# Gathers with a bound: leaving out the rows of dropped choices in a two-layer convolution kernel

## The chip, the core and the metric

The kernel runs on one core of a Trainium2 chip. The metric is the device time of one execution in microseconds (us). Before the change it is 5500.93 us, the median of three runs (5497.88 to 5509.63). The profiled execution took 5513.8 us. In the profile PE is TensorE's matrix products and PEld its weight loads, DVE is VectorE, ACT is ScalarE, POOL is GpSimd and SP is SyncE; L853 is line 853 of the kernel.

## What is computed

The input x has 32 images of 128 channels and 56 x 56 pixels, all in float32. Layer 0 is a depthwise 7 x 7 convolution, a normalisation over the channels, and a mixture of experts over all 32 x 3136 = 100,352 pixels ("tokens"). Layer 1 is a dilated 3 x 3 convolution followed by two-dimensional Fourier transforms, an attention over channels and a gate. What matters here is how layer 0 drops work and how its result comes back (the reference, cut):

```python
logits = xf @ Wg + bg
topv, topi = jax.lax.top_k(logits, 2)            # two experts of eight for each token
wts = jax.nn.softmax(topv, axis=-1)
order = jnp.argsort(-wts[:, 0])                  # the surest tokens come first
cap = int(1.25 * T / 8)                          # 15,680 rows for each expert
...
keep = pos < cap                                 # pos: place of the choice in its expert's queue
slot = jnp.where(keep, tiF * cap + pos, E * cap) # a dropped choice points past the end
...
yf = jnp.concatenate([y.reshape(E * cap, C), jnp.zeros((1, C), y.dtype)], axis=0)
contrib = yf[slot] * gate[:, None]               # there stands a row of zeros
...
return input + x_skip + moe_out                  # layer 1 starts from this sum
```

There are 200,704 choices and at most 8 x 15,680 = 125,440 are kept, so at least 37.5% of the choices are dropped and add nothing.

## The kernel before, in words

The work goes in three stretches.

In the first one (about 0 to 965 us) TensorE computes the depthwise convolution, VectorE and ScalarE normalise, and the router's logits and choices are made. The normalised tokens go to a table xf in HBM, in row blocks: a row block is eight image rows of two images, seven columns of 128 tokens, and there are 112 of them.

In the second one (about 965 to 3250 us) the experts run one after the other. For each expert VectorE makes the list of its tokens, GpSimd gathers their rows from xf (L674, tile xg, 128 rows each and 64 in the last gather of an expert, since 15,680 = 122 x 128 + 64), TensorE and ScalarE compute the two dense layers, and SyncE stores the gated rows in a table yf in HBM. Beside that VectorE adds up, for every token, where its two rows stand in yf: slot1 and slot2. They begin at NSLOT = 125,440, and a choice that is dropped keeps that value. yf has NSLOT + 1 rows, and the last one is zero (zrow, L389 to L391).

In the third one (from about 3250 us) layer 1 runs over 16 pairs of images. For each pair `front` builds the input of layer 1 and its convolution, and `back` does the transforms, the attention and the gate of the pair before. TensorE alternates between them: after each piece of `back` the driver draws pieces of `front` in proportion to the work done, beginning after the first sixth of `back` (LEAD, L1139). A pair has NB = 7 row blocks, and a row block goes through three small functions:

- `gather(r)` loads the 896 x 128 values of xf (tile xs, one plain load on SyncE's queue), and gathers the rows of yf that slot1 and slot2 name, into two tiles y of 128 x 7 x 128. A gather takes one column of 128 indices and fetches 128 rows of 512 bytes, so a row block has 14 of them, and the whole stretch has 112 x 14 = 1568 (L853). They are all issued by GpSimd, one after the other.
- `total(r)` adds both y tiles to xs on VectorE (L867).
- `place(r)` turns xs to channel-first on TensorE (L875) and adds it to the padded input image xp on VectorE (L880).

`feed(rb)` calls place for its own block, total for the next one and gather for the block three ahead. The tiles y come from a pool of four buffers, so two row blocks are in flight, and the gathers of block r + 2 must wait until `total(r)` has read its y tiles. A program that lays out the instructions on each engine keeps every engine's instructions in one fixed order, and each engine waits in that order. So an instruction that waits holds up all that stand behind it on its engine. ScalarE's instructions in this stretch are the Gelu of the convolution (feat, L906), the evacuations of transform results from PSUM (T at L945, Q at L1020), squares, roots and absolute values (sr, si, oa, ob), and one small root for the attention (nrm, L989).

Of the kernel before, what the change touches and what calls it, by code (L numbers as in the profile page):

```python
# [29 lines left out]
F32 = mybir.dt.float32  # L30
# [7 lines left out]
C = 128  # L38
# [12 lines left out]
NB = H // P8  # L51
# [20 lines left out]
def conv_seq_kernel(ctx: ExitStack, tc: tile.TileContext, t: dict, out: bass.AP, dbg: dict):  # L72
    nc = tc.nc
# [4 lines left out]
    NSLOT = E * cap  # L78
# [5 lines left out]
    dram = ctx.enter_context(tc.tile_pool(name="dram", bufs=1, space=DRAM))  # L84
# [15 lines left out]
    nc.vector.memset(eps6, 1.0e-6)  # L100

    xf = dram.tile([J * 128, PITCH], F32, name="xf")
    yf = dram.tile([NSLOT + 1, C], F32, name="yf")
    xfv = xf.rearrange("(j p) c -> p j c", p=128)


# [7 lines left out]
    with tc.tile_pool(name="a1", bufs=1) as a1, tc.tile_pool(name="a2", bufs=2) as a2, tc.tile_pool(  # L114
        name="a3", bufs=3
# [214 lines left out]
        for g in range(HI // 2):  # L330
            y = a2.tile([128, TG, C], F32, name="y")
# [31 lines left out]
    with tc.tile_pool(name="b1", bufs=1) as b1, tc.tile_pool(name="b2", bufs=2) as b2, tc.tile_pool(  # L363
        name="c1", bufs=1
# [21 lines left out]
            )  # L386
            nc.vector.tensor_tensor(out=b2v[:, e], in0=b2v[:, e], in1=lsB, op=ALU.mult)

        zrow = c1.tile([1, C], F32, name="zrow")  # L389
        nc.vector.memset(zrow, 0.0)  # L390
        nc.sync.dma_start(out=yf[NSLOT : NSLOT + 1, :], in_=zrow)  # L391

        blocks = b1.tile([128, U, NC], F32, name="blocks")
        for u in range(U):
            nc.vector.tensor_scalar(
                out=blocks[:, u, :], in0=iota[:, :NC], scalar1=float(-u), scalar2=None, op0=ALU.add
# [4 lines left out]
            out=token, in0=iota, scalar1=-128.0, scalar2=128.0, op0=ALU.add, op1=ALU.mult  # L401
# [440 lines left out]
    rows = {}  # L842

    def gather(r):
        if r >= NRB:
            return
        xs = d3.tile([128, NB, C], F32, name="xs")
        nc.sync.dma_start(out=xs, in_=xfv[:, r * NB : (r + 1) * NB, :C])
        ys = []
        for s in (slot1, slot2):  # L850
            y = d4.tile([128, NB, C], F32, name="y")
            for m in range(NB):
                nc.gpsimd.indirect_dma_start(  # L853
                    out=y[:, m, :],
                    out_offset=None,
                    in_=yf,
                    in_offset=bass.IndirectOffsetOnAxis(ap=s[:, r * NB + m : r * NB + m + 1], axis=0),
                )
            ys.append(y)
        rows[r] = xs, ys  # L860

    def total(r):
        if r >= NRB:
            return
        xs, ys = rows[r]
        for y in ys:
            nc.vector.tensor_tensor(out=xs, in0=xs, in1=y, op=ALU.add)  # L867

    def place(r, xps):
        xs, rb = rows.pop(r)[0], r % NB  # L870
        for m0 in range(0, NB, 4):
            nm = min(4, NB - m0)
            pt = bank("pxs")
            for m in range(nm):
                nc.tensor.transpose(pt[:, m * 128 : (m + 1) * 128], xs[:, m0 + m, :], ident)  # L875
            pv = pt[:, : nm * 128].rearrange("p (m i r s) -> p i r m s", m=nm, i=2, r=P8)
            for i in range(2):
                px = interior(xps[i], rb * P8, P8)[:, :, m0 * P8 : (m0 + nm) * P8]
                px = px.rearrange("p r (m s) -> p r m s", m=nm)
                nc.vector.tensor_tensor(out=px, in0=px, in1=pv[:, i], op=ALU.add)  # L880

    def front(pr, xps, feat):


        for i in range(2):
            nc.sync.dma_start(out=xps[i], in_=t["xp"][pr + i * HI])

        def feed(rb):
            r = pr * NB + rb
            place(r, xps)  # L890
            total(r + 1)
            gather(r + 3)

        def taps(pf, g, k0):
            for k in range(k0, k0 + 3):
                o = ((k // 3) * 3 + 8 * g) * RP + (k % 3) * 3
                for i in range(2):
                    nc.tensor.matmul(  # L898
                        pf[i * DD : (i + 1) * DD, : 8 * W],
                        lhsT=cw[:, k, :],  # L900
                        rhs=xps[i][:, o : o + 8 * RP].rearrange("p (h w) -> p h w", w=RP)[:, :, :W],
                        start=(k == 0),
                        stop=(k == 8),
                    )
            if k0 == 6:
                nc.scalar.activation(  # L906
                    feat[:, 8 * g * W : 8 * (g + 1) * W], pf[:, : 8 * W], AF.Gelu, scale=bsc, bias=bsh
                )

        feed(0)  # L910
        yield NB * 64
        for g in range(NB):
            if g + 1 < NB:
                feed(g + 1)
                yield NB * 64
            pf = psumf.tile([128, 512], F32, name="pf")
            for k0 in (0, 3, 6):
                taps(pf, g, k0)
                yield 3 * 8 * W


# [219 lines left out]
    for r in range(3):  # L1141
        gather(r)
# [9 lines left out]
    for w in front(0, *this):  # L1152
        pass
    for pr in range(NI // 2):
        then, steps = None, iter(())
        if pr + 1 < NI // 2:
            then = pair()
            steps = front(pr + 1, *then)
        made = fed = 0
        for w in back(pr, *this):  # L1160
            made += max(w, 0)
            goal = max(0, made - LEAD) * FRONT // (MAIN - LEAD)
            if w < 0:
                goal = max(goal, fed - w * 3 * 8 * W)
            while fed < goal:
                f = next(steps, None)
                if f is None:
                    break
                fed += f
        for w in steps:  # L1170
            pass
        this = then
# [137 lines left out]
```

## Time and profile before

| stretch, us | what runs | PE busy | ACT busy | POOL busy |
|---|---|---|---|---|
| 0 to 965 | depthwise convolution, routing | 664.17 | 467.99 | 11.44 |
| 965 to 3250 | experts | 2012.97 | 683.39 | 963.78 |
| 5367 to 5513.8 | end of the last pair | 123.31 | 78.14 | 0.20 |

The stretches between, 3250 to 5367 us, hold layer 1 with its gathers. They are shown word for word in the prediction. Busy time is the time in which an engine works on an instruction; the page's groups give for each kind of instruction its line, engine, operation, tile and number, then busy time and the mean duration of one in ns, and after the second bar the idle time of the engine just before these instructions with what ended it. "Issue" there means that the engine waited for nothing that the profile shows.

The software queue that carries the gathers is shown among the DMA queues as q0, with 81,664 packets and 175.18 MB in the whole execution: 103 MB of y rows and 72 MB of xg rows. Over the whole span TensorE is busy for 84%, VectorE for 56%, GpSimd for 47% and ScalarE for 38%.

### The profile page before, as it was taken

Reading aid. Unit: us, or ns where it says so; the run is one execution under the profiler, and the core shown is the slowest. Engines: PE = TensorE matmul, PEld = TensorE weight load, DVE = VectorE, ACT = ScalarE, POOL = GpSimd, SP = SyncE. Lnnn points to the kernel's source line nnn. Section 1 sums busy time; section 2 is a strip of 40 time slices with the busy share of each in tenths; the row PEclk is TensorE's granted clock in tenths of the full one; section 3 lists DMA queues with packets and bytes.
Section 4 is the critical chain, followed back from the end, with each engine's and each line's share of the span. In section 5 each row is a group of like instructions: output and inputs, shape, how many; then the busy total and the mean of one; then the engine's idle time right before and its main releaser. Section 6 shows DMA issues by size and latency. Waiting matters only on the chain.

```text
span 5513.8 us, 85629 instructions
## 1 busy us (share of the span) xinstructions
PE 4653.0 (84%) x32850; PEld 3226.8 (59%) x32850; DVE 3073.9 (56%) x6927; ACT 2097.5 (38%) x3595; POOL 2613.8 (47%) x2564
## 2 busy tenths in 40 slices
PE   6777675189988989899999965899999999899898
PEld 6666554166666667667776743555555555555556
DVE  4767776746565656454453322555555555555556
ACT  2544556023322323233333310444444444444445
POOL 0000000053535343445454447777777777777770
PEclk9888887589999999999999987999999999999999
DMA  9999995222222222222222243444444444444441
GB/s 258 247 242 244 241 233 132 50 66 60 69 54 66 57 62 61 63 66 71 69 70 73 73 120 74 118 126 127 123 123 124 125 123 123 125 128 125 123 121 42
DMA packets 616217, 634.09 MB, mean 115 GB/s; under 512 B 166145, under 2 KB 540546, under 8 KB 611714
## 3 DMA queue, kind: packets, MB, share of 16 engines
q1 hardware_dynamic: 332418, 395.64, 25.6%
q0 software_dynamic: 81664, 175.18, 14.8%
q10 hardware_dynamic: 201728, 57.81, 5.4%
q8 instruction: 260, 4.26, 0.3%
q14 instruction: 147, 1.20, 0.1%
HBM read 454.98 MB, written 173.41 MB: 114 GB/s over the span
## 4 chain that ended last, share of the span: by engine, by line
POOL 28%; PE 25%; issue 19%; DVE 7%; DMA 6%; ACT 2%; ACTq 0%; POOLq 0%; DVEq 0%; SPq 0%
POOL y L853 17%; POOL xg L674 10%; PE py L718 6%; PE ph L708 5%; PE pf L898 4%; PE pm L942 4%; DMA xg<-xf,ids 3%; DMA y<-yf,slot 2%; PE pt L934 2%; PE pg L966 1%; ACT y L181 1%; PE psa L136 1%; PE pxt L680 1%; DVE junk L419 1%; DVE y L187 1%
## 5 line engine op out<-in xcount | busy, mean ns | idle before, releaser
L853 POOL DMA_INDIRECT y<-yf,slot x1568 | 1638.6, 1045 | 527.7 <-issue 501.0
L674 POOL DMA_INDIRECT xg<-xf,ids x984 | 963.8, 979 | 1338.4 <-PE pxt L680 490.0
L711 ACT ACTIVATE hT<-ph,b1t 128x512 f32<-128x512 f32 (+1 forms) x992 | 676.1, 682 | 1428.8 <-PE ph L708 1402.6
L718 PEld LDWEIGHTS py<-W,hT 128*128 128x128 f32 x7872 | 950.8, 195 | 224.7 <-issue 155.1
L718 PE MATMUL py<-W,hT 128*128 128x128 f32 x7872 | 998.2, 281 | 75.4 <-DVE yo L731 69.8
L708 PE MATMUL ph<-xT,W 128*128 128x512 f32 (+1 forms) x1984 | 903.9, 595 | 0.2 <-DVE xT L694 0.2
L898 PE MATMUL pf<-xp,cw 128*64 128x448 f32 x4032 | 885.9, 566 | 0.9 <-DVE xp L880 0.8
L867 DVE TENSOR_TENSOR xs<-xs,y 128x896 f32<-128x896 f32 x224 | 244.4, 1091 | 644.7 <-DMA y<-yf,slot 591.9
L898 PEld LDWEIGHTS pf<-xp,cw 128*64 128x64 f32 x4032 | 289.0, 141 | 465.9 <-issue 439.7
L708 PEld LDWEIGHTS ph<-xT,W 128*128 128x128 f32 x1984 | 359.9, 193 | 336.4 <-issue 329.7
L136 PE MATMUL psa<-xt,wt 112*64 112x98 f32 x8192 | 413.1, 262 | 83.2 <-DMA wt<-in_wt_dram 74.9
L685 DVE SCALAR_TENSOR_TENSOR gat<-xg 128x4 f32<-128x4 f32 (+2 forms) x256 | 42.1, 164 | 785.0 <-DMA xg<-xf,ids 782.4
L136 PEld LDWEIGHTS psa<-xt,wt 112*64 112x64 f32 x8192 | 389.4, 146 | 121.4 <-issue 67.0
L936 DVE COPY mid<-pt 112x512 f32<-112x512 f32 (+3 forms) x480 | 305.3, 660 | 229.7 <-PE pt L934 229.0
L290 POOL MEMSET meta<- 128x1568 f32 x8 | 11.2, 1404 | 887.1 <-DMA xf<-meta 451.5
L181 ACT ACTIVATE y<-y,nb,sd 128x128 f32<-128x128 f32 x784 | 307.9, 482 | 119.1 <-issue 70.2
L945 ACT COPY T<-pm 128x464 f32<-128x464 f32 (+2 forms) x240 | 124.7, 520 | 404.7 <-PE pm L942 404.7
L144 DVE TENSOR_TENSOR y<-psa,dwbB 128x392 f32<-128x392 f32 x256 | 142.7, 563 | 232.8 <-PE psa L136 232.7
L731 DVE TENSOR_TENSOR yo<-py,b2t 128x512 f32<-128x512 f32 (+2 forms) x256 | 169.8, 666 | 112.1 <-PE py L718 111.3
L198 PE MATMUL pyt<-ident,y 128*128 128x128 f32 x784 | 137.8, 347 | 92.0 <-DVE nb L174 57.9
L680 PE MATMUL pxt<-ident,xg 128*128 128x128 f32 (+1 forms) x984 | 195.2, 280 | 11.0 <-DMA xg<-xf,ids 10.8
L1033 PE MATMUL pim<-feat,meanw 128*128 128x448 f32 x224 | 126.4, 651 | 92.2 <-ACT gt L1088 92.2
(376 smaller groups left out, 6185.1 us busy)
## 6 DMA issues: line engine op xcount, KB each, us to landing
xt<-in_x_dram SPq DMA_DIRECT2D x128, 784.0 KB
yf<-yo SPq DMA_DIRECT2D x240, 256.0 KB
xp<-in_xp_dram SPq DMA_DIRECT2D x32, 1832.0 KB
wt<-in_wt_dram SPq DMA_DIRECT2D x128, 448.0 KB
xs<-xf SPq DMA_DIRECT2D x112, 448.0 KB
xf<-y ACTq DMA_DIRECT2D x48, 1024.0 KB
y<-yf,slot POOLq DMA_INDIRECT x1568
out_dram<-oa SPq DMA_DIRECT2D x224, 112.0 KB
```

The lines of the kernel that those rows point to most:

```text
L136: nc.tensor.matmul(ps[h * 64 : (h + 1) * 64, c * TG : (c + 1) * TG], lhsT=wt[:, c4 + c, b, :], rhs=xv[:, c4 + c, h, :, b * NB : b * NB + N ...
L181: nc.scalar.activation(yi, yi, AF.Identity, scale=sd[:, i : i + 1], bias=nb[:, i : i + 1])
L674: nc.gpsimd.indirect_dma_start(out=xg[:n, q, :], out_offset=None, in_=xf, in_offset=bass.IndirectOffsetOnAxis(ap=ids[:n, c0 + q : c0 + q + ...
L680: nc.tensor.transpose(pt[:, q * 128 : q * 128 + n], xg[:n, q, :C], ident[:n, :n])
L708: nc.tensor.matmul(ph[:, :ns], lhsT=W1[:, e, f * C : (f + 1) * C], rhs=xT[:, :ns], start=True, stop=True)
L711: nc.scalar.activation(hT[:, f, :ns], ph[:, :ns], AF.Gelu, bias=b1t[:, e, f : f + 1])
L718: nc.tensor.matmul(py[:n, q * C : (q + 1) * C], lhsT=hT[:, f, q * 128 : q * 128 + n], rhs=W2[:, e, f, :], start=(f == 0), stop=(f == FF // ...
L853: nc.gpsimd.indirect_dma_start(out=y[:, m, :], out_offset=None, in_=yf, in_offset=bass.IndirectOffsetOnAxis(ap=s[:, r * NB + m : r * NB + ...
L867: nc.vector.tensor_tensor(out=xs, in0=xs, in1=y, op=ALU.add)
L898: nc.tensor.matmul(pf[i * DD : (i + 1) * DD, : 8 * W], lhsT=cw[:, k, :], rhs=xps[i][:, o : o + 8 * RP].rearrange("p (h w) -> p h w", w=RP) ...
L936: dve(mid[:m, :ni, :].rearrange("p i c -> p (i c)"), pt[:m, : ni * 128])
L942: nc.tensor.matmul(pm[:, i * M : (i + 1) * M], lhsT=mid[:m, i, :], rhs=by, start=True, stop=True)
```

## The change

The gathers of layer 1 get a bound. An index above NSLOT - 1, which is what a dropped choice has, fetches nothing and leaves the row of y as it was. The purpose is that rows of dropped choices are not fetched. Since y is a reused buffer, the row must be zero beforehand, and ScalarE writes zeros to the whole tile ahead of its seven gathers. yf loses its row of zeros, and the store of that row goes. The call of `gather` is moved out of `feed`: for the third block ahead it now comes one step after the first feed of a pair, and otherwise after the first three taps of a convolution group, so that the clear is queued later on ScalarE.

```diff
-    yf = dram.tile([NSLOT + 1, C], F32, name="yf")
+    yf = dram.tile([NSLOT, C], F32, name="yf")
...
-        zrow = c1.tile([1, C], F32, name="zrow")
-        nc.vector.memset(zrow, 0.0)
-        nc.sync.dma_start(out=yf[NSLOT : NSLOT + 1, :], in_=zrow)
...
             y = d4.tile([128, NB, C], F32, name="y")
+            nc.scalar.memzero(y)
             for m in range(NB):
                 nc.gpsimd.indirect_dma_start(
                     out=y[:, m, :],
                     out_offset=None,
                     in_=yf,
                     in_offset=bass.IndirectOffsetOnAxis(ap=s[:, r * NB + m : r * NB + m + 1], axis=0),
+                    bounds_check=NSLOT - 1,
+                    oob_is_err=False,
                 )
...
             place(r, xps)
             total(r + 1)
-            gather(r + 3)
...
         feed(0)
         yield NB * 64
+        gather(pr * NB + 3)
         for g in range(NB):
...
             for k0 in (0, 3, 6):
                 taps(pf, g, k0)
+                if k0 == 0 and g + 1 < NB:
+                    gather(pr * NB + g + 4)
                 yield 3 * 8 * W
```

The clears are 224 instructions on ScalarE, each over 128 partitions x 896 values. In the built program each gather also has a register move ahead of it on GpSimd, which holds the bound, and each clear waits for the additions and the gathers that used its buffer before.

## The prediction

> **What bounds the kernel now.** I read the page first, then busy time by stretch, then the timeline of single instructions. The costliest group of the page is the row gather of layer 1:
>
> ```profile
> L853 POOL DMA_INDIRECT y<-yf,slot x1568 | 1638.6, 1045 | 527.7 <-issue 501.0
> ```
>
> 1568 gathers of 1.045 us, and idle time of which 501 of 528 us is "issue": GpSimd waited for nothing. The answer for the tile y puts them between 3250.2 and 5366.3 us. With the last one's 0.94 us that is 2117 us, or 1.350 us per gather. The timeline of GpSimd shows what that is made of:
>
> ```profile
> 4520.43 0.94 POOL L853 DMA_INDIRECT y<-yf,slot  x1 [0.30 <-DVE xp L880]
> 4521.67 0.94 POOL L853 DMA_INDIRECT y<-yf,slot  x1 [0.30 <-issue]
> 4522.92 0.94 POOL L853 DMA_INDIRECT y<-yf,slot  x1 [0.30 <-issue]
> 4524.17 1.25 POOL L853 DMA_INDIRECT y<-yf,slot  x1 [0.30 <-issue]
> 4525.72 0.94 POOL L853 DMA_INDIRECT y<-yf,slot  x1 [0.30 <-issue]
> 4526.97 1.25 POOL L853 DMA_INDIRECT y<-yf,slot  x1 [0.30 <-issue]
> ```
>
> Second column: us of one; in brackets: idle time before it. 0.94 and a gap of 0.30, over and over: 1568 x 1.249 = 1958 us; the other 159 us are the longer ones (1.25 and more). No gap waits for data, so GpSimd is saturated through this stage, and what it feeds waits for it. The list of waits, from 3430 to 5367 us, leads with that:
>
> ```profile
> DVE xs L867 <- DMA y<-yf,slot: 444.0, 128, 7.3
> POOL y L853 <- issue: 409.3, 1343, 0.3
> ```
>
> VectorE stands 444 us for gathered rows. The second limit is close. Busy time by stretch (columns: length, then PE, PEld, DVE, ACT, POOL):
>
> ```profile
> 3250.00:3430.00 180.00, 86.45 (x393) 44.55 (x393) 32.14 (x51) 7.25 (x11) 137.12 (x141) 0.71 0.38 95
> 3430.00:5367.00 1937.00, 1766.07 (x10729) 1068.10 (x10729) 1089.74 (x1921) 860.71 (x1344) 1501.29 (x1428) 0.96 0.49 124
> ```
>
> TensorE is at 1766 of 1937 us, 91%, ScalarE at 44%, the DMA engines at 49%. So layer 1 is bound by the pace of the gathers, with TensorE some 9% behind.
>
> [...] 0.94 us every time, while the addition that waits for the last gather (which ends at 5367.2) starts 1.9 us later, at 5369.14. So fetching fewer bytes shortens nothing by itself; only a shorter instruction does. [...] the 1.25 us gathers of the fence lie beside additions of L867 (at 4523.50 and 4526.31 us), which have two SBUF inputs.
>
> **The change, part by part.**
>
> Rows not fetched. There are 32 x 3136 = 100,352 tokens with two choices, 200,704 in all; eight experts keep at most 15,680 each, 125,440. At least 75,264 are dropped, 37.5%, 48 of the 128 rows of a gather. Today they all read the zero row. What do 48 rows cost GpSimd? The gather of layer 0 (L674) has eight instances of 64 rows, the last of each expert; one stands here behind a full one:
>
> ```profile
> 2451.68 0.95 POOL L674 DMA_INDIRECT xg<-xf,ids  x1 [0.30 <-issue]
> 2452.93 0.90 POOL L674 DMA_INDIRECT xg<-xf,ids  x1 [0.30 <-issue]
> ```
>
> For this tile the trace gives 903 ns as the least and 944 as the median: 41 ns for 64 rows, 0.64 ns a row. Over 860 of 944 ns don't depend on rows at all. If dropped rows leave the descriptor lists, a gather saves 48 x 0.64 = 31 ns, all on the path: 1568 x 31 ns = 48 us. If they stay as empty descriptors it saves nothing.
>
> The bound itself. Each row's index must be compared; no row of the trace shows what that costs. Lower end 0: at 0.64 ns a row [...] one more comparison vanishes. [...] I take 0 for the forecast[...].
>
> A register move ahead of each gather. The changed program has 1568 of them in GpSimd's stream, for the bound. Nearest row: a semaphore instruction ahead of a gather (17 to 43 ns) leaves its gap at 0.30, as in the fence (the gather at 4520.43, released by DVE). The sequencer works ahead during the 0.94 us; I take 0. At 43 ns unhidden it would be 67 us.
>
> The clears. 224 of 128x896 on ScalarE, an Identity activation from SBUF to SBUF. Nearest row: L1046, SBUF to SBUF, 576 ns for 448 elements a partition; L945 has 534 ns for 448 and 252 for 112, so 0.84 ns an element; 576 + 448 x 0.84 = 0.95 us. 224 x 0.95 = 213 us of ScalarE, which goes from 44% to about 55% of the stage. It hides in ScalarE's idle time, which is waits for TensorE.
>
> The new wait. A gather waited for the additions that freed its buffer (VectorE); now a clear waits for them, and the gather for the clear. Behind a waiting clear stand ScalarE's evacuations of PSUM (T, Q, feat), and TensorE waits for those. Four y buffers hold two row blocks, so the buffer of block r+2 comes free while GpSimd issues block r+1, 14 x 1.35 = 19 us. The tightest place comes once in a pair, where the front stage pauses. An instance:
>
> ```profile
> 4123.00 1.09 DVE L867 TENSOR_TENSOR xs<-xs,y 128x896 f32<-128x896 f32 x1 [0.99 <-DMA y<-yf,slot]
> 4125.81 1.08 DVE L867 TENSOR_TENSOR xs<-xs,y 128x896 f32<-128x896 f32 x1
> ...
> 4130.85 0.94 POOL L853 DMA_INDIRECT y<-yf,slot  x1 [0.30 <-issue]
> ...
> 4119.03 0.30 ACT L989 ACTIVATE nrm<-nrm,eps 128x1 f32<-128x1 f32 x1
> 4126.19 0.55 ACT L1020 COPY Q<-pm 128x464 f32<-128x464 f32 x1 [6.86 <-PE pm L942]
> ```
>
> The first buffer is free at 4124.1; in the changed order its clear stands between the nrm and Q of ScalarE, so it can run from 4124.1 to 4125.1, 5.8 us before the gather that needs it. The second is wanted seven gathers later. A delay of Q by up to 2 us a pair is inside TensorE's 9%. Cost taken: 0.
>
> Emitting the gather later (after the first taps) and some swapped neighbours on TensorE and VectorE: GpSimd's own order is as before, 0. Bytes: y loses 37.5%, hidden, since the DMA engines are half idle. The zero row and its write: one small store, 0.
>
> Sum: -48 us, 5501 - 48 = 5453.
>
> **The rivals.**
>
> Empty descriptors, and a free comparison: nothing on the path moves, 5501. For it: the 860 ns that don't depend on rows. [...]
>
> The comparison costs: [...] For it: saturated GpSimd passes on each ns 1568 times[...]. Against: the 0.64 ns a row. This one ends slower.
>
> The clears become the wait: if the tight place of each pair lost about 3.5 us (a clear that stands behind a late evacuation), 16 x 3.5 = 56, 5557. Against it: the 5.8 us above.
>
> A gather much shorter, so that TensorE bounds: with TensorE at 97% instead of 91% the long stretch takes 1766 / 0.97 = 1821 us, 116 less: 5385. Nothing shows that much to be saved.
>
> **How the numbers follow.** Shorter by the rows' share 0.42 (5453); nothing moves 0.13 (5501); the comparison costs 0.32[...]; the clears 0.07 (5557); TensorE bounds 0.06 (5385). Faster 0.42 + 0.06 = 0.48, same 0.13, slower 0.39. The range goes from 5390 to 5760: it leaves out the lower half of the last case (0.03) and the tail of the costly comparison, a gather longer by over 165 ns (about 0.12).
>
> **What would show it.** In the profile after, the group of the gathers decides: a usual duration of about 0.91 us and a mean near 1.01 is the forecast, 0.94 the first rival, above 0.98 the second; the gap tells whether the register move hides (0.30) or not. Waits of GpSimd for ScalarE, or of TensorE for a clear, would show the third. Over 1.1 us for one would make the prediction wrong outright.

## The result, and the profile after

After the change the kernel takes 5591.57 us (median, 5588.42 to 5594.5). The kernel before took 5499.68 us beside it (5497.88 to 5509.63). The ratio is 1.0163, with an interval of 1.0146 to 1.0181: **slower by 92 us**. The forecast was 5453. The time lies inside the range, on the side of the second rival.

The two groups of the page that answer to the gathers of before, and the new clears (busy us, mean ns; then idle time ahead of them and what ended it):

```profile
L852 POOL DMA_INDIRECT y<-yf,slot x1568 | 1717.9, 1096 | 526.8 <-issue 474.1
L850 ACT ACTIVATE y<-y 128x896 uint32<-128x896 uint32 x224 | 212.4, 949 | 504.5 <-DVE xs L868 486.4
```

The gathers were to become shorter and have become longer: a mean of 1096 ns, where before had 1045. Their busy time rose by 79.3 us, from 1638.6 to 1717.9, while the idle time ahead of them stayed (526.8, before 527.7). The answer for the tile y gives minimum, median and maximum in ns, then the first and the last start:

```profile
L852 POOL DMA_INDIRECT y<-yf,slot x1568: 992/997/2493, 3247.1 to 5441.4; - x196
```

The usual gather went from 944 to 997 ns. From the first start to the end of the last one it is now 2195.3 us instead of 2117.0, which is 78.3 more. What follows the last gather hardly changed (147.6 us, before 146.6). So the stretch whose pace the gathers set holds the whole difference between the two profiled executions (5590.0 - 5513.8 = 76.2 us; the profiled one of before was some 15 us above its median, so the medians differ by more).

The timeline of GpSimd, at the place that the prediction showed of before (start, us of one, idle time before it in brackets):

```profile
4521.42 1.00 POOL L852 DMA_INDIRECT y<-yf,slot  x1 [0.30 <-issue]
4522.72 0.99 POOL L852 DMA_INDIRECT y<-yf,slot  x1 [0.30 <-issue]
4524.02 1.00 POOL L852 DMA_INDIRECT y<-yf,slot  x1 [0.30 <-issue]
4525.32 1.00 POOL L852 DMA_INDIRECT y<-yf,slot  x1 [0.30 <-ACT ob L1125]
4526.62 1.45 POOL L852 DMA_INDIRECT y<-yf,slot  x1 [0.30 <-DMA y<-yf,slot]
```

The form is the old one: back to back, a gap of 0.30, now and then a longer one. Only the 0.94 has become 1.00. Two releasers are named here that are no "issue", but the gap with them is the same 0.30, so they cost nothing.

Busy time by stretch (length, then PE, PEld, DVE, ACT, POOL, then the granted clock, the share of the DMA engines and GB/s):

```profile
3430.00:5367.00 1937.00, 1735.93 (x10292) 1051.65 (x10294) 1053.29 (x1853) 998.05 (x1492) 1518.10 (x1376) 0.94 0.36 101
```

The same 1937 us hold 1376 GpSimd instructions instead of 1428 and 10,292 matrix products instead of 10,729: everything advances at the slower pace of the gathers. ScalarE went from 44% to 52%. The DMA engines fell from 49% to 36%, and the queue of the gathers shows why:

```profile
q0 software_dynamic: 81664, 136.94, 9.5%
```

It moved 38 MB less than the 175.18 of before, so the rows really are not fetched. Its packets are as many as before: 81,664, which is 32 for each of the 1568 + 984 gathers. That alone doesn't tell whether a dropped row is left out, since the eight gathers of 64 rows among the 984 have 32 packets as well. The bytes do. All y rows are 200,704 x 512 bytes = 102.76 MB, so 72.42 MB of this queue are not y rows. With 125,440 kept rows (64.22 MB) that makes 136.64. The 0.30 MB that remain are 4 bytes for each of the 75,264 dropped rows. A dropped row becomes an entry of 4 bytes; it is not left out.

The list of waits (us in total, times, longest), from 3430 to 5450 us:

```profile
DVE xs L868 <- DMA y<-yf,slot: 400.5, 102, 8.3
POOL y L852 <- issue: 387.5, 1272, 0.3
ACT y L850 <- DVE xs L868: 325.6, 123, 8.7
```

VectorE still stands for gathered rows, as before. The third line is new: clears that wait for the additions. What that does is looked at below, with the point on the clears in the account of the prediction.

### The profile page after: what moved, and what is told of

Read it like the earlier page. It is cut to its first block, busy times and chain, and to the rows that moved or that the text cites. A ratio compares the mean times of both kernels' runs of the same rounds, so it can differ in the third digit from the quotient of the medians.

```text
span 5590.0 us, 88259 instructions
## 1 busy us (share of the span) xinstructions
PE 4690.1 (84%) x32850; PEld 3254.8 (58%) x32850; DVE 3073.9 (55%) x6926; ACT 2290.9 (41%) x3819; POOL 2691.0 (48%) x2564
## 3 DMA queue, kind: packets, MB, share of 16 engines
q0 software_dynamic: 81664, 136.94, 9.5%
## 5 line engine op out<-in xcount | busy, mean ns | idle before, releaser
L852 POOL DMA_INDIRECT y<-yf,slot x1568 | 1717.9, 1096 | 526.8 <-issue 474.1
L898 PE MATMUL pf<-xp,cw 128*64 128x448 f32 x4032 | 903.1, 568 | 0.5 <-DVE xp L881 0.5
L850 ACT ACTIVATE y<-y 128x896 uint32<-128x896 uint32 x224 | 212.4, 949 | 504.5 <-DVE xs L868 486.4
L937 PE MATMUL pt<-ident,T 128*112 128x128 f32 (+1 forms) x912 | 152.5, 302 | 73.3 <-ACT T L948 63.1
```

What stands on the lines that cost most here:

```text
L850: nc.scalar.memzero(y)
L852: nc.gpsimd.indirect_dma_start(out=y[:, m, :], out_offset=None, in_=yf, in_offset=bass.IndirectOffsetOnAxis(ap=s[:, r * NB + m : r * NB + ...
L898: nc.tensor.matmul(pf[i * DD : (i + 1) * DD, : 8 * W], lhsT=cw[:, k, :], rhs=xps[i][:, o : o + 8 * RP].rearrange("p (h w) -> p h w", w=RP) ...
L937: nc.tensor.transpose(pt[:m, i * 128 : (i + 1) * 128], src(i0 + i), ident)
```

## The experiments

Each is compared with the kernel before, run beside it on the same chip. The table sums up those that change one gather. "Excess" is busy time less 1568 times the usual duration, so the longer gathers alone; the fifth column is 1568 x (mean - 1.045 us).

| kernel | usual ns | mean ns | excess, us | from the mean, us | measured, us |
|---|---|---|---|---|---|
| before | 944 | 1045 | 158 | | |
| clears, no bound | 944 | 1052 | 170 | +11 | +12 |
| bound and drops, no clears | 997 | 1085 | 138 | +63 | +66 |
| bound alone | 997 | 1092 | 149 | +74 | +73 |
| after | 997 | 1096 | 155 | +80 | +92 |
| bound, error mode | 1013 | 1105 | 144 | +94 | +90 |
| all rows dropped | 997 | 1128 | 205 | +130 | +130 |
| adding gathers | 1541 | 1573 | 51 | +828 | +782 |

The last two columns agree to within 12 us, but for the last row (explained there): in this stretch the added time of the gathers comes out as time of the kernel.

The traces tell what the longer gathers stand beside. Among VectorE's instructions of this stretch, the additions of `total` and a number of others (TENSOR_TENSOR) read two operands from SBUF, the memory that holds the tiles. By the start and end times in all fourteen traces, 4396 gathers of y rows took over 50 ns more than the usual one of their run, and each of them overlaps such an instruction. Of the 13,517 gathers that overlap none, not one is longer than usual by more than 28 ns. Beside the additions of `place` (L880), which have one operand in PSUM, where TensorE's products land, none is lengthened unless one of the others overlaps it too.

### The bound alone

The kernel before, with a bound that no index exceeds; nothing is cleared or dropped.

```diff
+                    bounds_check=NSLOT,
+                    oob_is_err=False,
```

> The kernel before, with a bound of NSLOT on the gathers of layer 1, so that the zero row stays in range and nothing is dropped; no clears, same places. Theory A (the bound costs a fixed 53 ns a gather, dropped rows give nothing back, clears and later places cost nothing): usual gather 0.997 us, mean near 1.098, 1568 x 53 ns = 83 us, 5583 us. Theory B (the bound costs 84 ns and the 48 dropped rows gave 31 back): 1.028 us, 5500 + 132 = 5632. Theory C (handling dropped rows costs, 1.1 ns each, and the test nothing): 0.944 us, 5500. Theory D (a part of the 92 us is the clears and their wait): a time clearly below 5583 though the gather is at 0.997.

Measured: 5590.56 against 5517.09 us, a ratio of 1.0135 (1.0115 to 1.0156). The answer for the tile y of this kernel:

```profile
L853 POOL DMA_INDIRECT y<-yf,slot x1568: 992/997/2494, 3238.2 to 5427.3; - x196
```

The 53 ns are there in full, to the ns, with not one row dropped. q0 moved its 175.18 MB. So the bound has a price of its own, and the dropped rows give nothing back: 997 with 37.5% dropped, 997 with none.

### The clears without the bound

The changed kernel, its row of zeros back and the two lines of the bound gone.

```diff
-                    bounds_check=NSLOT - 1,
-                    oob_is_err=False,
```

> The changed kernel without the bound: the zero row is back and fetched, ScalarE still clears each y and the gathers still wait for the clears and stand at the later place. Theories A, B and C: gather 0.944 us, 5500 us within 12. Theory D: gather 0.944 us but 5515 us or more, with gaps before gathers that wait for ScalarE.

Measured: 5529.16 us, 1.0028 (1.0019 to 1.0037).

```profile
L856 POOL DMA_INDIRECT y<-yf,slot x1568: 940/944/2493, 3260.5 to 5389.9; - x196
```

The usual gather is at 944 again. The 12 to 15 us that remain aren't waits for a clear: the idle time ahead of the gathers sums to 529.8 us against 527.7. They are longer gathers (excess 170 against 158), and 8 of these us lie beside the additions of `total` (89 against 81). With the bound's 1.35% these 0.28% make 1.63%, the whole change to within the intervals.

### The bound with dropped rows, without the clears

The kernel before with the bound at NSLOT - 1, each of the four buffers cleared once at its first use. Later rows of dropped choices hold what was there, so the output differs; the work is the same.

```diff
+            if r < 2:
+                nc.scalar.memzero(y)
...
+                    bounds_check=NSLOT - 1,
+                    oob_is_err=False,
```

> The kernel before, with the bound of NSLOT - 1, so that dropped rows are not fetched, at the old place and with clears of the first four buffers only; a dropped row keeps what the buffer held, so it adds an old row. Theories A and B: gather 0.997 us, 5583 us, the same as the changed kernel within 12. Theory C the same. Theory D: below the changed kernel by more than 12 us.

Measured: 5582.94 us, 1.0118 (1.0097 to 1.0138), with a usual gather of 997 ns. It is no slower and no faster than the bound alone, within their intervals. Rows that aren't fetched save nothing, with or without clears.

### All rows dropped

The changed kernel with the bound at 0, so that layer 1 gets next to none of the experts' sum.

```diff
-                    bounds_check=NSLOT - 1,
+                    bounds_check=0,
```

> The changed kernel with a bound of 0, so that nearly every row of the gathers of layer 1 is dropped and adds zero. Theory A: gather 0.997 us whatever is dropped, 5590 us. Theory B: 84 - 128 x 0.64 = +2 ns, gather 0.946 us, about 5510. Theory C: 944 + 128 x 1.1 = 1085 ns, 5500 + 221 = 5721.

Measured: 5647.2 us, 1.0236 (1.0211 to 1.0261). All was dropped: q0 moved 73.22 MB, which is the 72.42 that are not y rows and 4 bytes for each of the 200,704 rows. The packet records show it one by one: a gather's rows go in 16 packets of eight rows, each of 4096 bytes before, and all but one of these 25,088 packets have 32 bytes here. And the usual gather still takes 997 ns:

```profile
L852 POOL DMA_INDIRECT y<-yf,slot x1568: 992/997/2497, 3251.7 to 5496.1; - x196
```

This settles the share of the rows at zero. That the kernel became slower still was not foreseen. The timelines of GpSimd and VectorE show where:

```profile
3903.51 1.00 POOL L852 DMA_INDIRECT y<-yf,slot  x1 [0.30 <-DMA y<-yf,slot]
3903.92 1.09 DVE L868 TENSOR_TENSOR xs<-xs,y 128x896 f32<-128x896 f32 x1 [1.32 <-DMA xs<-xf]
...
3912.94 1.09 DVE L868 TENSOR_TENSOR xs<-xs,y 128x896 f32<-128x896 f32 x1 [2.93 <-DMA y<-yf,slot]
3913.19 1.71 POOL L852 DMA_INDIRECT y<-yf,slot  x1 [0.31 <-issue]
...
3933.09 1.09 DVE L868 TENSOR_TENSOR xs<-xs,y 128x896 f32<-128x896 f32 x1 [2.74 <-DMA y<-yf,slot]
3933.18 1.87 POOL L852 DMA_INDIRECT y<-yf,slot  x1 [0.31 <-issue]
```

The first gather starts ahead of the addition and keeps its 1.00; the other two start while an addition runs, and are longer. The excess is 205 us instead of 155, and the whole of the 50 us lies beside the additions (129 us of excess there, after the change 78). More gathers now start while an addition runs, 194 instead of 146. That they do so because the data land sooner is likely, but argued and not shown.

### The bound on the experts' gathers

The kernel before with a bound that no index exceeds on the gathers of layer 0 (L674), where GpSimd is not saturated (963.78 us busy of 2285 before).

```diff
+                    bounds_check=J * 128 - 1,
+                    oob_is_err=False,
```

> The kernel before, with a bound on the gathers of the experts' stretch (tile xg) alone; every index is in range. If the bound is a fixed price of an instruction, the usual xg gather goes from 0.944 to 0.997 us and its 64-row instances from 0.903 to 0.956; if it is a price per row (0.41 ns), the 64-row ones go to 0.930. GpSimd waits for TensorE and VectorE in this stretch, so 984 x 53 ns = 52 us more work on it should cost nothing: ratio to before 1.000 within 0.002. If the price of the bound reached the end wherever it is paid, the ratio would be 1.009.

Measured: 5545.54 against 5522.89 us, 1.0048 (1.0032 to 1.0063), where no change was expected. The answer for the tile xg, whose minimum is a gather of 64 rows and whose median is one of 128:

```profile
L674 POOL DMA_INDIRECT xg<-xf,ids x984: 942/997/1790, 1123.7 to 3230.8; - x197
```

Before it was 903/944. So the bound costs 39 ns on 64 rows and 53 on 128. On a straight line through these two points that is 0.22 ns a row and 25 ns a gather whatever the rows. In the list of waits from 1000 to 3250 us one sees how the price reached the end although GpSimd idles:

```profile
DVE gat L687 <- DMA xg<-xf,ids: 813.5, 224, 7.6
POOL xg L674 <- PE pxt L682: 600.9, 197, 9.3
```

Before, these two were 782.4 and 490.0. A chunk's four gathers come one after the other, what uses their rows waits for the last, and GpSimd in turn waits longer for TensorE to release its buffer. In this chain the price is latency: of 984 x 53 ns = 52 us, 21 showed as a longer stretch from the first xg gather to the last (2087.4 to 2108.1 us).

### The bound in error mode

The kernel before with a bound that no index exceeds, in the mode that reports a row above the bound and doesn't skip it.

```diff
+                    bounds_check=NSLOT,
+                    oob_is_err=True,
```

> As the run with the bound only (bound NSLOT, nothing out of range), but an index out of range would be an error instead of being skipped. If the comparison or the register that holds the bound is what costs: gather 0.997 us, ratio 1.013 to 1.016. If the ability to skip is what costs: 0.944 us, ratio 1.000.

Measured: 5613.32 us, 1.0154 (1.0135 to 1.0173).

```profile
L853 POOL DMA_INDIRECT y<-yf,slot x1568: 1006/1013/2490, 3263.1 to 5472.7; - x196
```

69 ns instead of 53. So the price isn't that of being able to skip; it comes with the bound in both modes. What the 53 ns and the 69 ns consist of was not separated.

### Half the gathers

The kernel before with the rows of slot1 alone: 784 gathers, and the second choice's part left out of the sum. It asks how far behind TensorE is. VectorE has 112 additions fewer as well, and the four y buffers now hold four row blocks instead of two, so what it saves is not the gathers' time alone.

```diff
-        for s in (slot1, slot2):
+        for s in (slot1,):
```

> The kernel before without the gathers and the addition for the second choice, so that its part of the sum is left out: 784 gathers instead of 1568. If GpSimd's pace is the only limit close by, layer 1 would halve; TensorE at 91% must stop it far earlier. By the busy time of TensorE, at 97% of the long stretch: 116 us less, and up to 90 us less in the first 180 us, where TensorE is at 48%: ratio 0.963 to 0.980. If layer 1 is not bound by the gathers at all: 1.000.

Measured: 5197.78 us, 0.9418 (0.9401 to 0.9434): 325 us less, well beyond what was expected. Busy time of the stretch from 4000 to 4500 us, first of the kernel before:

```profile
4000.00:4500.00 500.00, 455.83 (x2735) 268.63 (x2733) 287.15 (x505) 229.35 (x358) 387.54 (x367) 0.96 0.47 120
```

and then of this one:

```profile
4000.00:4500.00 500.00, 496.83 (x3186) 311.13 (x3183) 290.98 (x534) 246.84 (x389) 223.48 (x210) 1.00 0.43 113
```

TensorE went from 91% to 99% busy, 9% more, but did 3186 products instead of 2735, 16% more. The busy time of its weight loads rose with the work (268.63 to 311.13, 16%), that of its products did not. A product by name, the group of the convolution's products in the same window, before and in this kernel: 563 and 545 ns. Now the pace is set elsewhere; the waits from 3430 to 5000 us are led by

```profile
POOL y L853 <- DVE xs L867: 624.2, 63, 24.6
```

GpSimd waits for buffers, which it didn't before. So the busy share of the products, 91%, did not tell how much more work TensorE could take. The weight loads, at 54% of the stretch before (268.63 of 500) and 62% in this kernel, grew as the work did. How near 62% is to their limit no run here shows.

### Adding in the gather

The gathers add their rows to xs themselves, and VectorE's additions and the tiles y go. xs has six buffers, loaded two blocks ahead.

```diff
-                    out=y[:, m, :],
+                    out=xs[:, m, :],
...
+                    compute_op=ALU.add,
```

> The kernel before, but the gathers add their rows to xs themselves (accumulate in the DMA), with six xs buffers loaded two blocks ahead; no y tiles and no additions on VectorE. If an accumulating gather keeps its 0.944 us and gap of 0.305 us, and the longer gathers that come from VectorE's additions go (some 75 of the 159 us beyond 1568 x 1.249): ratio 0.986, 75 us less. If the accumulating form is longer by 50 ns a gather, that is taken back: 1.000. If it must wait for the landing of the first choice's rows: gaps before gathers and slower.

Measured: 6304.44 us, 1.1415 (1.1399 to 1.1431).

```profile
L855 POOL DMA_INDIRECT xs<-yf,slot x1568: 1532/1541/2122, 3253.4 to 6196.4; - x196
```

A gather that adds takes 1541 ns, 597 more. The queue had 257,280 packets: 984 x 32 + 1568 x 144, so 144 for an adding gather instead of 32: 128 of one row each, and 16 of 4 bytes. The stretch of the gathers grew by 828 us, as the means say; 40 of it came back in the tail, presumably since TensorE was less behind by then (106.6 us after the last gather, before 146.6). With the additions of `total` gone from VectorE the excess is 51 us instead of 158; before, 81 us of it lay beside them.

### The additions on TensorE

Two kernels, each run on two chips. In the first both additions of a row block are done as accumulating products with the identity, in the place of the transposition; in the second one of the two.

```diff
-                nc.tensor.transpose(pt[:, m * 128 : (m + 1) * 128], xs[:, m0 + m, :], ident)
+                parts = [xs] + ys[0:]        # second kernel: ys[1:]
+                for k, part in enumerate(parts):
+                    nc.tensor.matmul(
+                        pt[:, m * 128 : (m + 1) * 128], lhsT=part[:, m0 + m, :], rhs=ident,
+                        start=(k == 0), stop=(k == len(parts) - 1),
+                    )
```

> The kernel before, but the two additions of gathered rows leave VectorE: TensorE, which turns xs to channel-first anyway, turns both y tiles too and sums the three in PSUM (1568 more products of 128x128; six y buffers). No bound. If the gathers' time beyond 1568 x 1.249 us (159 us) comes to a good half from VectorE's two-input additions, as the e8 run suggests (there 50 us were left), the mean gather falls from 1.045 to about 0.98 us: 1568 x 0.065 = 100 us less, and TensorE, which had 320 us to spare in the run with half the gathers, has to take 1568 x 0.156 = 245 to 440 us more: ratio 0.982 if that fits, 1.000 to 1.02 if TensorE becomes the limit.

> As the run with both additions on TensorE, but only the second choice's rows go there (784 more products, 122 to 220 us of TensorE), the first choice's are still added by VectorE. Half of the collisions go: some 50 us less, ratio 0.991, and TensorE stays within its spare time. If two-input additions are not what lengthens the gathers: 1.000.

> Both additions on TensorE, once more, on a chip where the kernel before takes about 5500 us (on the last one it took 6345 us, with TensorE's granted clock at 0.88 in the profile, so that TensorE and not GpSimd set the pace). The mean gather should be 0.988 us as there, 57 ns less than before: 1568 x 0.057 = 89 us less if TensorE keeps up, ratio 0.984. If 1568 further products (504 us by the last profile for both y tiles' 3136 products... of which half, 1568, are for one tile) exceed the 320 us that TensorE had to spare: ratio 1.00 to 1.03, with GpSimd waiting for the products that free y.

> One addition on TensorE, once more, likewise. 1568 more weight loads and products... in fact 784 columns, about 220 to 345 us of TensorE by the last profile, against 320 us to spare: ratio 0.990 if it fits and half of the collisions go, 1.000 to 1.015 if TensorE becomes the limit.

Measured: both, 6635.15 us, 1.0449 (1.0421 to 1.0476), and again 6628.88, 1.0466 (1.044 to 1.0492); one, 6423.07, 1.0126 (1.0094 to 1.0158), and again 6417.04, 1.0122 (1.0096 to 1.0147). On the two chips of these runs the kernel before itself took about 6340 us (6345.54 and 6338.24), at a mean granted clock of 0.87 instead of 0.92. No profile of it was taken there, so why it is some 840 us slower is not known. The waits of the first kernel from 4000 to 6000 us, in its second run, are led by

```profile
POOL y L854 <- PE pxs L879: 722.1, 46, 34.7
```

GpSimd waits for TensorE, so the gathers no longer set the pace. And TensorE got more work than the text of the kernel suggests: an accumulating product of this form counts as two in the trace (1568 for xs alone, where the transposition had 784). The first kernel has 3920 products more than the 32,850 of before and the second 2352, where 1568 and 784 had been reckoned with. TensorE was busy for 81% of these 2000 us, and some waits of VectorE and ScalarE have no releaser in the trace that is known, so that the added products are what costs the time is likely, not shown. For the question asked, whether a VectorE free of additions shortens the gathers and thereby the kernel at its usual pace, the four runs are inconclusive. The mean gather with no addition was 993 ns, but with GpSimd idle half of the time that isn't comparable; with one addition it was 1051 and 1045 ns, no shorter than before. No version was found that computes the whole and beats the kernel before.

## Why the prediction was wrong

**Rows not fetched: 48 us were forecast to be saved, and nothing was.** The prediction took 31 ns off a gather, from the 64-row instances. Measured is 0: 997 ns with none, 37.5% and all rows dropped. The figure of 0.64 ns a row was measured on gathers with fewer indices (903 ns for 64, 944 for 128); a dropped row keeps its index and its entry, of 4 bytes. The prediction named this ("If they stay as empty descriptors it saves nothing") and gave it too little: that a row without a transfer leaves no entry was the author's guess, which no trace had shown. The step that failed is the one from "fewer rows asked for" to "fewer rows".

**The bound itself: the term taken as 0 measures 53 ns.** 1568 x 53 ns = 83 us, 0 was forecast. The argument was that at 0.64 ns a row one more comparison vanishes; that was an estimate, since the trace of before has no gather with a bound. The price did not vanish: by the line through the two row counts (39 ns at 64, 53 at 128) it grows by 0.22 ns a row, which is 28 ns at 128 rows, and over 1568 gathers 44 us. Nor did the argument see the fixed part of that line, 25 ns and 39 us, which no difference between row counts can show. The second rival had it right that the bound costs; how much, no trace of before shows. With 53 ns it would have given 5501 + 83 = 5584, 8 us from the result. Whether it is the comparison that costs, as it supposed, is open. The range of the forecast holds the result because of this rival, not by the forecast's own mechanism.

**GpSimd as the limit: right.** The table of experiments follows from it: what the mean gather loses times 1568 comes out as time.

**The register move: right.** The trace has one of 29 ns ahead of each gather; the gap is still 0.30, the sum of idle time 526.8 us. The sequencer does work ahead: the last move starts at 5433.1 us, 8.3 us before the last gather (5441.4).

**The clears: right in size, wrong on what they hold up.** They take 949 ns (0.95 forecast), 212.4 us together, and no gather waits for one longer than its gap of 0.30. But the prediction expected the clear at the tight place to stand behind the nrm and to delay Q by up to 2 us a pair. Here is what happens once in a pair, in the timelines of VectorE, ScalarE and TensorE after the change:

```profile
4240.77 1.09 DVE L868 TENSOR_TENSOR xs<-xs,y 128x896 f32<-128x896 f32 x1 [7.74 <-DMA y<-yf,slot]
...
4241.95 0.95 ACT L850 ACTIVATE y<-y 128x896 uint32<-128x896 uint32 x1 [7.51 <-DVE xs L868]
4242.81 0.23 ACT L948 COPY T<-pm 128x112 f32<-128x112 f32 x1
...
4243.09 2.82 PE L937 MATMUL pt<-ident,T 128*116 128x128 f32 x12 [5.16 <-ACT T L948]
```

The addition waits 7.74 us for its rows, the clear waits for the addition, T, whose products ended at 4235.53, stands behind the clear on ScalarE until 4242.81, and TensorE waits 5.16 us for T. In the waits from 3430 to 5360 us it comes 14 times:

```profile
PE pt L937 <- ACT T L948: 61.8, 14, 5.4
```

The kernels before and with the bound alone have no such line. So the chain that the third rival feared exists, and is longer than thought. It costs next to nothing all the same, presumably because TensorE's margin takes it: the kernel with clears and no bound has these waits too (43.2 us, 14 times) and lost 0.28%, and its page puts that on longer gathers (11 us), not on waits. What moves VectorE's additions so that more of a gather's time falls beside them isn't settled; both the clears and the later call of `gather` may, and no run separates the two.

**Bytes: right.** 38 MB less, from 49% to 36% of the DMA engines, and no us for it.

**TensorE some 9% behind: mis-sized.** The last rival let it bound at a supposed 97%, 116 us below before. With half the gathers the kernel ran 325 us faster, and at 99% busy TensorE did 16% more products. Its busy share was the wrong measure.

## What to carry to other kernels

Runs without an option can't show what the option costs, and a fixed price shows in no comparison of two sizes (here the 25 ns of the line): ahead of a change that puts an option on a saturated instruction, measure one with the option and no effect. Saving bytes is worth nothing where the pace is set by issuing the gathers, as it was here (38 MB less, and not a ns off the gather); ask whether the dropped work leaves the list or stays in it as an empty entry. And a wait put on an engine's in-order queue is to be judged by what stands behind it there (here T, and TensorE's 5.16 us), even if the instruction that was meant to wait never does.

## What the runs showed of the hardware

- A bound on an indirect gather cost 53 ns at 128 rows, with none, 37.5% or all of the rows dropped, 39 ns at 64 rows with none dropped, and 69 ns at 128 in error mode.
- A dropped row left the number of packets as it was (81,664) and moved 4 bytes; it gave GpSimd no time back (997 ns in each case).
- A gather was lengthened (by up to 1.5 us in the kernels before and after) only beside VectorE instructions with two operands in SBUF: 4396 of 4396 in fourteen traces, 158 us of 1639 in the kernel before.
- A gather that adds to its destination took 1541 ns instead of 944, with 144 packets instead of 32.
- An off-path price reached the end: GpSimd was busy for 42% of the experts' stretch (963.78 of 2285 us), and a price of 52 us there cost the kernel 0.48%.
- A TensorE 91% busy did 16% more products in the same time with half the gathers gone, at a clock of 1.00 instead of 0.96.
